# A decoder layer in float32: the bias of attention's output as one more product of TensorE

## The chip, the cores and the metric

The kernel runs on one core of a Trainium2 chip. Its time is the device time of one execution in microseconds. Before the change three runs took 5265.96, 5266.59 and 5273.14 us; the median, 5266.59, is what the changed kernel is compared with. The engines are named as in the profile: PE is TensorE (its weight loads are PEld), DVE is VectorE, ACT is ScalarE, POOL is GpSimd, SP is SyncE, whose queue issues most transfers.

## The reference, cut to what matters

```python
x = layernorm(x + mamba(x))                       # selective scan, 1024 channels, 16 states
x = layernorm(x + attention(x, ctx, mask))        # 16 heads of 32
x = layernorm(x + experts(x))                     # 32 routed experts and a shared MLP

# the end of attention, for each of 8 batches (512 rows of 512)
out = out.transpose(0, 2, 1, 3).reshape(B, L, D_MODEL)
return out @ Wo.T + bo
```

All is float32. x has 8 batches of 512 rows and 512 columns. In the mamba part, dt = softplus(dt @ dt_proj_w + dt_proj_b) with dt of rank 32, and dt_proj_w is 32 x 1024. The values' bias bv of attention adds a constant row to every row of the attention result, since the softmax weights of a row sum to one; so the kernel leaves bv out of the values and adds bv @ Wo.T to bo once.

## The kernel before, in words

The function `layers` computes the first two parts and the routing, `experts` the routed experts, `finish` the last layernorm. The change is all in `layers`.

The scan runs chunk by chunk: 16 chunks of 256 rows, two to a batch, 32 steps to a chunk. A step takes four channel groups of a state group: DVE multiplies (`steps_in`, L494, 128x1024), scans (`scan`, L501) and multiplies by C (`collect`, L510); ACT makes the decays ahead (`decays`, L480, four activations, a quartet, into one of two buffers `das`); PE folds the states (`products`, L521) into `py`, begun by a product with the identity (L519), and DVE gates the result (`gated`, L535). Six `h` buffers go round: a new step's L494 needs the fold products of the sixth step before it. Beside these steps other work is placed: the projections of the next chunk (`project`, L343), its convolution (L363 and L369 on ACT, L377 on DVE), the dt product (`prepare`, L437, with `w_dt`), x_proj (L400), and attention, routing and shared MLP of the batch before (`units`).

`units(b)` lists the parts of attention for batch b with weights, and the step loop takes them from the list in proportion, so that the attention of batch b lies beside the scan of batch b+1. A part is a product on PE and a rest that follows on another engine when the next part has been issued. The framework's scheduler then fixes the order of the instructions on each engine when the program is built; each engine works its own list in order. The last batch's attention stands alone behind the scan.

The part that the change touches is `output(lt)`, four for each batch. `dense` makes a 128x512 product of four 128x128 pieces of `attT` and `Wo` (L756) in one of two PSUM buffers. Then DVE adds the residual (L919, into `xr`) and the bias, which has been broadcast to all 128 partitions (L920, into `x2t`). After the fourth, layernorm 3 follows: statistics on DVE (L62, L63, L65), a logarithm and an exponential on ACT (L69, L70), a Newton step on DVE (L74 to L79), and the normalization on ACT (L81). PE transposes the result (`flip2`, L932), ACT copies it (L933), and the products of the shared MLP (L756, from `x2T`) and of the router (L588) follow. The residual rows are fetched two tiles ahead of use into two buffers `xr`.

Once, near the start (step 2 of the first chunk), `biases` makes bv @ Wo.T: L1051 repeats bv, L1052 multiplies, and L1055 adds the product to `bo`, which L278 has loaded with a broadcast to 128 partitions. SP's queue at that time issues, in this order: the spill of B and C (`scr`, L408), the clearing of the experts' buffer `xbuf` (L258, 1.36 MB each, one of many), the broadcasts of B and C (`bc`, L418), the repeats of dt and of dt times x (`rep`, L428).

Of the kernel before, what the change touches and what calls it, by code (L numbers as in the profile page):

```python
# [8 lines left out]
F32 = mybir.dt.float32  # L9
# [3 lines left out]
ALU = mybir.AluOpType  # L13
# [4 lines left out]
P = 128  # L18
B, S, D = 8, 512, 512
DC = D // P  # L20
# [3 lines left out]
DI = 1024  # L24
# [65 lines left out]
def layers(ctx, tc, a, x1d, filld, based, xbuf, arm):  # L90
# [42 lines left out]
    def const(name, shape, src):  # L133
        t = cp.tile(shape, F32, name=f"l_{name}")
        nc.sync.dma_start(t, src)
        return t
# [40 lines left out]
    cw = const("cw", [P, CC, 4], rows(a["conv_w"]))  # L177
    cb = const("cb", [P, CC], a["conv_b"])
    w_x = const("w_x", [P, CC, RANK + 2 * NST], rows(a["x_proj_w"]))
    w_dt = const("w_dt", [RANK, DI], a["dt_proj_w"])  # L180
    b_dt = const("b_dt", [P, CC], a["dt_proj_b"])
    dpar = const("dpar", [P, CC], a["D_param"])
    rs = const("rs", [P, 1], a["res_scale"].partition_broadcast(P))
    bq = cp.tile([P, DC], F32, name="l_bq")
    bk = cp.tile([P, DC], F32, name="l_bk")
    bv = cp.tile([P, DC], F32, name="l_bv")
    bo = cp.tile([P, D], F32, name="l_bo")
    wg = cp.tile([P, DC, E], F32, name="l_wg")

    aneg = cp.tile([P, CC, NQ, NG], F32, name="l_aneg")  # L190
# [72 lines left out]
    def later_constants():  # L263

        nc.sync.dma_start(
            aneg.rearrange("p c j g -> p (c j) g"),
            a["A_log"].rearrange("(b c) (s g) -> (c s) b g", c=QP, s=NQ),
        )
        for i in range(NPB):
            for r0 in (HD + 1, 2 * HD + HD + 1):  # L270
                nc.sync.dma_start(
                    kas[i][r0 : r0 + 1, :].rearrange("p (c t) -> p c t", c=DC),
                    ones[0:1, :].unsqueeze(1).to_broadcast([1, DC, P]),
                )
        nc.sync.dma_start(bq, a["bq"])
        nc.sync.dma_start(bk, a["bk"])
        nc.sync.dma_start(bv, a["bv"].rearrange("(c p) -> p c", p=P))
        nc.sync.dma_start(bo, a["bo"].partition_broadcast(P))  # L278
        nc.sync.dma_start(wg, rows(a["wg"]))


# [150 lines left out]
    def prepare(q, f):  # L432

        ps = psm.tile([P, 2, T], F32, tag="mm", name="ps_dt")
        for i in range(2):
            c = 2 * q + i
            nc.tensor.matmul(  # L437
                ps[:, i, :], w_dt[:, c * P : (c + 1) * P], f["xd"][0:RANK, :], start=True, stop=True
            )

        def exponentials():
            u = mp.tile([P, 2, T], F32, tag="u", name="u")
            dt = mp.tile([P, 2, T], F32, tag="dt", name="dt")

            for i in range(2):
                c = 2 * q + i
                nc.scalar.activation(u[:, i, :], ps[:, i, :], AF.Abs, bias=b_dt[:, c : c + 1])
                nc.scalar.activation(dt[:, i, :], ps[:, i, :], AF.Relu, bias=b_dt[:, c : c + 1])
            nc.scalar.activation(u, u, AF.Exp, scale=-1.0)
            l = mp.tile([P, 2, T + 3], F32, tag="xp", name="l")[:, :, 0:T]  # L450
            nc.scalar.activation(l, u, AF.Ln, bias=1.0)
            w = dtx = mp.tile([P, 2, T], F32, tag="dtx", name="dtx")
            nc.scalar.activation(w, u, AF.Identity, bias=1.0)

            def both():

                nc.vector.scalar_tensor_tensor(w, w, -1.0, u, ALU.add, ALU.subtract)
                nc.vector.tensor_tensor(l, l, w, ALU.subtract)
                nc.vector.tensor_tensor(dt, dt, l, ALU.add)
                nc.vector.tensor_tensor(dtx, dt, f["xs"][q], ALU.mult)  # L460
                f["ready", q] = dt, dtx
                return wait(timesD)

            def timesD():
                for i in range(2):
                    c = 2 * q + i
                    nc.scalar.activation(
                        f["xs"][q][:, i, :], f["xs"][q][:, i, :], AF.Identity, scale=dpar[:, c : c + 1]
                    )

            return wait(both)

        return exponentials
# [276 lines left out]
            todo.append((3.4, lambda j=j: keys(j), False))  # L750
        return todo

    def dense(lhs, rhs):
        ps = psm.tile([P, S], F32, tag="mm", name="ps_p")
        for dc in range(DC):
            nc.tensor.matmul(ps, lhs(dc), rhs(dc), start=(dc == 0), stop=(dc == DC - 1))  # L756
        return ps

    def units(b):
# [148 lines left out]
        def output(lt):  # L908
            if lt == 0:
                st["x2t"] = big("s1", "x2t").rearrange("p (j r) -> p j r", j=SC)  # L910
                st["x2"] = [st["x2t"][:, j, 0:D] for j in range(SC)]
            xr = st.pop(("xr", lt))
            if lt + 1 < SC:
                fetch(lt + 1)
            w, attT = loaded["Wo"], st["attT"]
            pp = dense(lambda dc: attT[:, dc, lt * P : (lt + 1) * P], lambda dc: w[:, dc, :])

            def add_up():
                nc.vector.tensor_tensor(xr, pp, xr, ALU.add)  # L919
                nc.vector.tensor_tensor(st["x2"][lt], xr, bo, ALU.add)  # L920
                if lt == SC - 1:
                    return layernorm(nc, sm, st["x2"], st["x2"], "ln3")

            return add_up
# [112 lines left out]
    def biases():  # L1037
# [12 lines left out]
        for dc in range(DC):  # L1050
# [1 line left out]
            nc.tensor.matmul(  # L1052
                psb, rep[:, dc * P : (dc + 1) * P], loaded["Wo"][:, dc, :], start=(dc == 0), stop=(dc == DC - 1)
            )
        nc.vector.tensor_tensor(bo, bo, psb, ALU.add)  # L1055

    chunks = [(b, t) for b in range(B) for t in range(S // T)]
    steps = [(q, g, jj) for q in range(CC // 2) for g in range(NG) for jj in range(2)]
# [584 lines left out]
```

## Time and profile before

| what | us |
|---|---|
| median of three runs | 5266.59 |
| the profiled execution | 5280.81 |
| its span | 5279.1 |
| scan phase, first step to the last scan | 58 to 3521 |
| attention, routing and shared MLP of the last batch, alone | to about 3800 |
| experts | about 3800 to 5240 |
| PE busy over the span | 4501.0 (85%) |
| DVE busy | 4173.3 (79%) |
| ACT busy | 2586.6 (49%) |
| L919, 32 adds | 21.8, 680 ns each |
| L920, 32 adds | 21.7, 678 ns each |

A row of the timeline gives the start, the time, the engine, the line, the operation, what it writes and reads, and how many instructions were merged; in square brackets stands the idle time of the engine before it and what ended it. PE records a float32 product twice: 128 products of `wa` and `attT` are 256 records. The answer by windows gives the busy time of each engine in a stretch and the share of full speed that PE's clock was granted.

### The profile page before, as it was taken

How to read it: one execution, taken by the hardware profiler on the slowest of the kernel's cores; microseconds unless marked ns; L12 is line 12 of the kernel's file. 1: busy time of each engine (PE TensorE's matmuls, PEld its weight loads, DVE VectorE, ACT ScalarE, POOL GpSimd, SP SyncE). 2: the span in 40 equal slices, each digit the busy share in tenths (PEclk: the TensorE clock that was granted, in tenths of full speed). 3: DMA queues.
4: the chain of work that ended last, by engine and by line, in shares of the span. 5: the costliest groups of instructions: out<-in, count | busy, mean ns of one | idle time of the engine just before them, and what ended most of it. 6: DMA issues, size and time to landing. Idle time of an engine off the chain costs nothing. (4 is left out here: it accounts for less than half of the span.)

```text
span 5279.1 us, 54371 instructions
## 1 busy us (share of the span) xinstructions
PE 4501.0 (85%) x17184; PEld 2464.4 (47%) x17184; DVE 4173.3 (79%) x5351; ACT 2586.6 (49%) x5771; POOL 588.5 (11%) x426
## 2 busy tenths in 40 slices
PE   6768889888888888888897888888899999999995
PEld 3324234333433433343342343332478888877774
DVE  7999898989989898998999899874355666656555
ACT  5565565665656556565655556533122333323233
POOL 1000002002000200200020020010112121111111
PEclk8879899999999999999999999999899999999997
DMA  8885345435533634544463554432244444444444
GB/s 236 266 229 157 72 119 177 115 101 148 160 95 91 208 88 109 171 128 102 105 201 78 125 173 113 106 115 93 93 129 125 128 139 132 128 116 132 117 123 151
DMA packets 486438, 711.64 MB, mean 135 GB/s; under 512 B 121576, under 2 KB 205064, under 8 KB 483952
## 3 DMA queue, kind: packets, MB, share of 16 engines
q1 hardware_dynamic: 449984, 626.90, 41.0%
q0 software_dynamic: 33280, 67.81, 5.8%
q10 hardware_dynamic: 2736, 11.54, 0.5%
q8 instruction: 221, 3.62, 0.3%
q14 instruction: 217, 1.78, 0.1%
HBM read 391.24 MB, written 164.79 MB: 105 GB/s over the span
## 5 line engine op out<-in xcount | busy, mean ns | idle before, releaser
L480 ACT ACTIVATE l_da<-rep,l_aneg 128x256 f32<-128x256 f32 x2048 | 893.5, 499 | 950.0 <-DVE h L501 885.6
L501 DVE TENSOR_TENSOR_SCAN h<-l_da,h 128x1028 f32<-128x1028 f32 x512 | 1163.3, 2285 | 21.6 <-ACT l_da L480 19.1
L494 DVE TENSOR_TENSOR h<-rep,bc 128x1024 f32<-128x1024 f32 x512 | 612.3, 1212 | 109.1 <-PE py L521 91.2
L510 DVE TENSOR_TENSOR h<-h,bc 128x1024 f32<-128x1024 f32 x512 | 616.8, 1211 | 2.1
L521 PE MATMUL py<-h,l_fold 128*32 128x512 f32 x2048 | 371.9, 649 | 108.1 <-DVE h L510 89.7
L819 PE MATMUL ps_s<-l_ka,l_qa 64*128 64x512 f32 x1024 | 331.8, 719 | 134.5 <-DVE mx L821 134.2
L1334 PE MATMUL ps_h<-xT,w 128*128 128x224 f32 (+3 forms) x1536 | 380.0, 397 | 38.4 <-issue 31.4
L1427 POOL DMA_INDIRECT based<-y,xe x160 | 272.5, 1703 | 1168.5 <-ACT y L1406 439.1
L821 DVE TENSOR_REDUCE mx<-ps_s 128x2 f32<-128x1024 f32 x256 | 309.8, 1214 | 67.8 <-PE ps_s L819 67.4
L861 PE MATMUL po<-eT,l_va 128*64 128x512 f32 x1024 | 302.5, 672 | 49.0 <-ACT eT L849 44.2
L1334 PEld LDWEIGHTS ps_h<-xT,w 128*128 128x128 f32 x1536 | 295.4, 193 | 103.8 <-issue 46.7
L845 PE MATMUL ps_t<-l_qa,l_ka 64*128 64x512 f32 x1024 | 305.5, 668 | 23.5 <-ACT eT L849 23.2
L849 ACT ACTIVATE eT<-ps_t 128x1024 f32<-128x1024 f32 x256 | 258.7, 1014 | 127.9 <-PE ps_t L845 127.8
L694 POOL DMA_INDIRECT xbuf<-x2t,dest x128 | 217.1, 1696 | 864.6 <-DVE dest L679 763.9
L343 PE MATMUL ps_z<-xnT,wm 128*128 128x256 f32 x1024 | 237.9, 389 | 28.4 <-DVE o L561 24.2
L756 PE MATMUL ps_p<-x2T,wa 128*128 128x512 f32 x512 | 241.9, 627 | 21.8 <-ACT hT L950 15.5
L552 PE MATMUL po<-wm,zs 128*128 128x512 f32 x512 | 248.5, 640 | 13.1 <-DVE z L963 11.8
L1334 PE MATMUL ps_h<-t,s 128*128 128x224 f32 (+3 forms) x1024 | 248.1, 393 | 5.8 <-DVE hT L1355 5.8
L1355 DVE TENSOR_TENSOR hT<-ps_h,p 128x224 f32<-128x224 f32 (+3 forms) x128 | 55.2, 432 | 248.9 <-PE ps_h L1334 248.8
L343 PE MATMUL ps_x<-xnT,wm 128*128 128x256 f32 x1024 | 245.7, 392 | 5.0 <-ACT xnT L332 3.2
L343 PEld LDWEIGHTS ps_z<-xnT,wm 128*128 128x128 f32 x1024 | 195.2, 193 | 90.2 <-DVE o L561 37.4
L343 PEld LDWEIGHTS ps_x<-xnT,wm 128*128 128x128 f32 x1024 | 195.8, 195 | 80.2 <-issue 43.7
(239 smaller groups left out, 6989.4 us busy)
## 6 DMA issues: line engine op xcount, KB each, us to landing
w<-in_w SPq DMA_DIRECT2D x93, 1024.0 KB
wm<-in_in_proj_w SPq DMA_DIRECT2D x128, 512.0 KB
rep<-dt SPq DMA_DIRECT2D x256, 256.0 KB
rep<-dtx SPq DMA_DIRECT2D x256, 256.0 KB
xbuf<-zero SPq DMA_DIRECT2D x32, 1362.5 KB
xe<-xbuf SPq DMA_DIRECT2D x32, 1362.5 KB
wm<-in_out_proj_w SPq DMA_DIRECT2D x64, 512.0 KB
wa<-in_sw SPq DMA_DIRECT2D x24, 1024.0 KB
```

Source lines behind the costliest of these rows:

```text
L343: nc.tensor.matmul(ps[:, i, :], w[:, dc, i * P : (i + 1) * P], f["xnT"][:, dc, :], start=(dc == 0), stop=(dc == DC - 1),)
L480: nc.scalar.activation(da[:, n, 1:], dt[:, j, i, :], AF.Exp, scale=aneg[:, 2 * q + i, 2 * jj + j, g : g + 1])
L494: nc.vector.tensor_tensor(h[:, :, 1:], dtx.rearrange("p j i t -> p (j i) t"), f["bc", g][0], ALU.mult)
L501: nc.vector.tensor_tensor_scan(flat, da.rearrange("p n t -> p (n t)"), flat, 0.0, ALU.mult, ALU.add)
L510: nc.vector.tensor_tensor(h[:, :, 0:T], h[:, :, 1:], f["bc", g][1], ALU.mult)
L521: nc.tensor.matmul(f["py"][j * QP : (j + 1) * QP, :, :], fold, hs[j // 2][:, 2 * (j % 2) : 2 * (j % 2) + 2, 0:T], start=False, stop=g == N ...
L819: nc.tensor.matmul(ps[:, j, :], qa[r, lt * P : (lt + 1) * P], ka[r, :], start=True, stop=True)
L821: return lambda: nc.vector.tensor_reduce(mx[:, lt, :].unsqueeze(2), ps, AX.X, ALU.max) and None
L845: nc.tensor.matmul(ps[:, j, :], ka[r, kc * P : (kc + 1) * P], qa[r, :], start=True, stop=True)
L861: nc.tensor.matmul(po[j * 2 * HD : (j + 1) * 2 * HD, :], va[:, kc, i, j * HD : (j + 2) * HD], eT[:, j, :], start=(kc == 0), stop=(kc == SC ...
L1334: nc.tensor.matmul(ps, w[:, n, r * P : (r + 1) * P], x[:, n, 0:cols], start=not more and n == 0, stop=n == 1, skip_group_check=more,)
L1427: put = nc.gpsimd.indirect_dma_start(out=based, out_offset=bass.IndirectOffsetOnAxis(ap=xe.bitcast(I32)[:, j, D + E :], axis=0), in_=ys[j] ...
```

## The change

The bias is no longer kept on 128 partitions. `w_dt`, the tile of dt's weights, grows from 32 to 64 partitions: the upper 32 hold dt's weights as before, the first of the lower 32 holds the bias of attention's output in 512 of its columns, and the other 31 are zero. In `dense`, a fifth product is added for the output: 32 rows of ones as the stationary operand and the 32 rows of bias and zeros as the moving one, accumulated into the same PSUM buffer. The add of the bias on DVE goes, and the residual add writes `x2t` directly. In `biases` the sum of bo and bv @ Wo.T is made on one partition of a buffer, and a transfer brings it to its row of `w_dt`, since DVE's lanes don't change partitions.

```diff
-    w_dt = const("w_dt", [RANK, DI], a["dt_proj_w"])
+    w_dt = cp.tile([2 * RANK, DI], F32, name="l_w_dt")
+    nc.sync.dma_start(w_dt[0:RANK, :], a["dt_proj_w"])
+    bo = w_dt[RANK : 2 * RANK, 0:D]
+    nc.gpsimd.memset(bo, 0.0)
...
-    bo = cp.tile([P, D], F32, name="l_bo")
...
-        nc.sync.dma_start(bo, a["bo"].partition_broadcast(P))
...
-                ps[:, i, :], w_dt[:, c * P : (c + 1) * P], f["xd"][0:RANK, :], start=True, stop=True
+                ps[:, i, :], w_dt[0:RANK, c * P : (c + 1) * P], f["xd"][0:RANK, :], start=True, stop=True
...
-    def dense(lhs, rhs):
+    def dense(lhs, rhs, row=None):
         ps = psm.tile([P, S], F32, tag="mm", name="ps_p")
         for dc in range(DC):
-            nc.tensor.matmul(ps, lhs(dc), rhs(dc), start=(dc == 0), stop=(dc == DC - 1))
+            nc.tensor.matmul(ps, lhs(dc), rhs(dc), start=(dc == 0), stop=(dc == DC - 1 and row is None))
+        if row is not None:
+            nc.tensor.matmul(ps, ones[RANK : 2 * RANK, :], row, start=False, stop=True)
         return ps
...
-            pp = dense(lambda dc: attT[:, dc, lt * P : (lt + 1) * P], lambda dc: w[:, dc, :])
+            pp = dense(lambda dc: attT[:, dc, lt * P : (lt + 1) * P], lambda dc: w[:, dc, :], bo)
 
             def add_up():
-                nc.vector.tensor_tensor(xr, pp, xr, ALU.add)
-                nc.vector.tensor_tensor(st["x2"][lt], xr, bo, ALU.add)
+                nc.vector.tensor_tensor(st["x2"][lt], pp, xr, ALU.add)
...
-        nc.vector.tensor_tensor(bo, bo, psb, ALU.add)
+        row = p3.tile([P, D], F32, tag="row", name="bo")[0:1, :]
+        nc.sync.dma_start(row, a["bo"].unsqueeze(0))
+        nc.vector.tensor_tensor(row, row, psb[0:1, :], ALU.add)
+        nc.sync.dma_start(bo[0:1, :], row)
```

## The prediction

> **What bounds the kernel now.** I read the chain of waits first; it only follows the last experts' transfers and the closing layernorm, after 5187 us, which the change doesn't touch. So I went on to the busy time by stages.
>
> ```profile
> core 0: us, PE busy (x) PEld busy (x) DVE busy (x) ACT busy (x) POOL busy (x), PEclk, DMA share, GB/s
> 58.00:460.00 402.00, 285.08 (x840) 121.90 (x840) 399.68 (x366) 240.87 (x591) 21.48 (x12) 0.79 0.79 231
> ...
> 1665.00:2118.00 453.00, 381.81 (x1381) 165.59 (x1381) 411.32 (x453) 266.92 (x595) 41.31 (x29) 0.94 0.47 129
> ...
> 3467.00:3700.00 233.00, 202.77 (x702) 74.97 (x700) 121.14 (x172) 76.93 (x119) 16.28 (x19) 0.92 0.32 105
> ```
>
> DVE bounds the scan phase: 91% busy in a full batch period (411.3 of 453 us) and 99% in the first, which has no attention output yet. After 3520 PE bounds. The output product of attention (lines 913 to 921) runs eight times: at 761, 1212, 1665, 2118, 2570 and 3023 us inside full periods, at 3467 near the end of the scan, at 3712 alone. Next, one of the six in the timeline, and the PE lines that give prices:
>
> ```profile
> 1666.31 0.68 DVE L920 TENSOR_TENSOR x2t<-xr,l_bo 128x512 f32<-128x512 f32 x1
> 1666.77 7.13 PE L756 MATMUL ps_p<-wa,attT 128*128 128x512 f32 x16
> 1666.91 0.68 DVE L919 TENSOR_TENSOR xr<-ps_p,xr 128x512 f32<-128x512 f32 x1
> ...
> 1671.33 0.69 DVE L919 TENSOR_TENSOR xr<-ps_p,xr 128x512 f32<-128x512 f32 x1 [0.74 <-DMA xr<-x1d]
> ...
> 1673.74 3.62 PE L343 MATMUL ps_x<-xnT,wm 128*128 128x256 f32 x16
> ...
> 1677.29 1.06 PE L521 MATMUL py<-h,l_fold 128*32 128x512 f32 x6
> ...
> 1683.49 0.16 DVE L74 TENSOR_TENSOR m<-v,r 128x4 f32<-128x4 f32 x1 [1.45 <-ACT r L70]
> ...
> 1687.36 2.93 ACT L81 ACTIVATE x2t<-x2t,less,r 128x512 f32<-128x512 f32 x4 [1.71 <-DVE less L79]
> 1688.22 1.97 PE L932 MATMUL ps_tr<-l_ident,x2t 128*128 128x128 f32 x8 [8.03 <-ACT x2t L81]
> ...
> 1695.66 3.60 PE L756 MATMUL ps_p<-x2T,wa 128*128 128x512 f32 x8
> 1699.10 3.65 PE L588 MATMUL ps_l<-l_wg,x2T 128*128 128x32 f32 x32
> ```
>
> See that PE stands idle for 8.03 us until layernorm 3 has normalized x2t; DVE, working through adds, statistics and scan steps in between, is what is late. And the eighth output, with nothing beside it:
>
> ```profile
> 3710.29 10.55 PE L756 MATMUL ps_p<-wa,attT 128*128 128x512 f32 x20 [3.73 <-DVE attT L900]
> ...
> 3717.44 0.69 DVE L919 TENSOR_TENSOR xr<-ps_p,xr 128x512 f32<-128x512 f32 x1 [1.11 <-PE ps_p L756]
> ...
> 3720.88 0.69 DVE L919 TENSOR_TENSOR xr<-ps_p,xr 128x512 f32<-128x512 f32 x1 [1.07 <-PE ps_p L756]
> 3721.60 0.69 DVE L920 TENSOR_TENSOR x2t<-xr,l_bo 128x512 f32<-128x512 f32 x1
> ```
>
> Here DVE waits for each product: PE is on the path.
>
> **Removed: 32 adds on DVE.** L920 starts at 1666.31 and the next instruction at 1666.91, so one takes 0.60 us of a full DVE queue (0.68 overlaps the next), four 2.4 us per output. xr is free one instruction earlier, so its next load (the 0.74 us wait) should no longer be waited for.
>
> **Added: 32 products on PE.** Each float32 product shows as two records (256 records for the 128 products of wa and attT). Eight such records take 1699.10 - 1695.66 = 3.44, so 0.43 each, and a product of 128x512 is 0.86; depth does not help (the 32-row products of L437 show 374 ns at 128x256, as L343's do). A change of array shape costs extra: 16 half-width records before L521 take 1677.29 - 1673.74 = 3.55 against 16 x 0.215 = 3.44, so 0.11. Into the 32-row shape and out: 0.86 + 0.22 = 1.08 us, 4.3 per output. Bounds: 0.86 with no price for the shape; above, L437's weight loads were preceded 52 times by an idle of 33.5 us in all that nothing ended ("issue" in the answer for that line), 0.64 each, so 0.86 + 1.28 = 2.14. I take 1.08, since L521 is the nearest row: a change of shape right behind 128x128 work.
>
> Against this change speaks the Trainium skill, TensorEngine Tiling (Array Packing), Key Properties: switching the tiling mode drains TensorE. The row agrees that switching isn't free, at 0.11. With the 166 ns constant of a warm matmul (TensorE: Matmul & The Clock Gate, Single matmul latency and the lines after) as the drain, an estimate is 1.19 per product, 4.8 per output instead of 4.3; the sum would move by 0.5 in the last output alone.
>
> **A full period, stepped through.** The order on each engine is fixed when the program is built; I use the changed program's order with the durations of this trace (1024-wide multiply 1.11, scan 2.2, convolution tap 0.40, statistics 0.60).
> PE: output 0 is whole at 1664.7, now with its bias at 1665.8; output 1 at 1667.9, output 2 at 1672.4, output 3 at 1676.9 (1673.7 before: four fold products, 1.0, move behind them). The 16 ps_x records end at 1680.4, then eleven fold products wait for nothing, to about 1684.
> DVE from 1665.3, in its new order: multiply (1666.4), add 0, tap, statistics, add 1 (1668.7, having waited 0.1 for PE), multiply, statistics, scan (1672.7), multiply, add 2 (1674.5), multiply, statistics, scan (1678.4), add 3 (1679.1), multiply, statistics, variance (1681.0; before 1681.2).
> ACT now has both quartets of decays ahead of the logarithm: second scan over at 1678.4, quartet 1.7, two table loads of 1.28 and two 0.2 activations: 1683.1, where it was 1683.5. DVE puts two multiplies into the Newton step and the taps behind it, so the shift `less` is out at 1686.2 instead of 1687.3: x2t starts 1.1 us earlier, and DVE has done 3 multiplies (3.3) more and 5 taps (2.0) less, so stands 1.1 + 1.3 = 2.4 us ahead. The gate of L535 comes at 1691.0 instead of 1694.0; PE's L519 waits for it, then the last transposes and their copy, so the shared MLP's first product starts at about 1693.4 instead of 1695.66: 2.2 ahead.
> I take 2.3 per period, six periods: -13.8. The lower bound is 1.1 (only x2t's lead survives), the upper 2.3 + 0.8 (see the transposes below).
> The 4.3 us on PE cost nothing here, because the 8.03 us wait hides them: PE is done at 1684, x2t comes at 1686.2. If that cover is used up, see rival 1.
>
> The wait also slows what follows it: eight L932 records take 1.97 us after the 8.03 us wait, and 1.14 at 3495.41, after 0.23. Whether the shorter wait cures that, no row shows: 0 to 0.8 per period, not in my sum. The skill's TensorE: Matmul & The Clock Gate, Part 1, has PE's clock halved after an idle window of about 3.4 us; with the 2 us left, that rule would add the whole 0.8 six times, a sum of -16.0 instead of -11.2.
>
> **The seventh output** (3467): DVE is ahead by the same 2.4, but the first add now waits about 1 us for the bias, and the order mixes in more scan steps; the gate logic ends earlier, x2t later. I take -1.5, from +2 (PE's lateness counts) to -4 (the scan's lead counts).
>
> **The eighth** (3712): four products of 1.08 go on the path, one add of 0.72 (3721.60 - 3720.88) off it, the other three adds lie in DVE's waits: +3.6; by the bounds +2.7 to +7.8.
>
> **The beginning.** The broadcast load of bo (256 KB) goes; a memset of 32x512 on POOL (0.55 by the neighbours of L241) comes, hidden, since POOL has nothing urgent until 16.7 us. Three steps are new on SP and DVE: the row's load stands behind the scr spill, needs filld's landing (issued at 33.99) and delays the xbuf clear and eight bc loads by one issue, 0.4; they themselves wait until 43.40 for scr. DVE's L1055 now waits for the row, and behind it is queued the product dtx whose transfers DVE idles for (10.41 us until 58.5). scr, issued at 39.55, let its readers go at 43.40; the row right behind it should land by 44, before L1055 is reached at about 46.7. The write-back to w_dt is issued behind all rep loads of that step, 0.5 on SP ahead of weight loads, and is read 700 us later. Without cover: the row's landing would go on the path, 1 to 3 us. The built order also differs in the first period, where DVE has only 2.3 us of slack in 402. I take +0.5 for all, -1 to +5.
>
> **Sum:** -13.8 - 1.5 + 3.6 + 0.5 = -11.2 us. The profiled execution took 5280.8, 14.2 above the median of 5266.6; taken off the median: **5255.4**.
>
> **Rivals.**
> 1. Slower: the bias product lands on the path in every period. Place: the last add, which DVE reaches at 1678.5. It decides from the price where output 3 is ready no earlier: 1673.7 - 1.0 + 4p = 1678.5, p = 1.45 us. For it: L437's 0.64 us gaps; PE is 84% busy, its slack in the new order is 2 us. Against: 0.11 at L521. At p = 2.14 output 3 comes 2.8 us late, the fold products as well, so h buffers are freed late: +0.5 net per period (2.8 - 2.3), +7.8 at the eighth, about +3 at the seventh: 3 + 3 + 7.8 + 0.5 = +14, 5281.
> 2. No gain that lasts: DVE's 9% idle time takes the place of the adds; the 2.4 us lead is lost at the next wait for PE's fold products (L494, 14.6 us in six waits in the list of waits of one period), because PE got 4.3 us more. For it: both engines are over 80% busy. Against: x2t and the MLP start earlier too. Time: 0 per period, +2.6 rest: 5269.
> 3. More than forecast: the transposes run in 1.14, so 3.1 per period, and -4 at the seventh: -18.6 - 4 + 3.6 + 0.5 = -18.5, 5248. For it: the shorter wait; against: PE's slack is used up by the bias.
> 4. The order of the first period costs DVE 5 us more, the rest as forecast: 5260.
>
> **How the numbers follow.** Forecast 0.48 (own range 5249 to 5261), rival 1 0.16, rival 2 0.15, rival 3 0.10, rival 4 0.11. No change is within 0.2%, 10.5 us, about what a measurement of this kernel can tell: 5256.1 to 5277.1. The forecast lies 0.7 us inside "faster"; I count two thirds of it there, since the transposes' gain is left out of it: 0.31, with rival 3 and a fifth of rival 4 0.43. Slower takes most of rival 1 (0.13) and a tail of rival 2 (0.03): 0.16. Same is the rest, 0.41. The range, 5246 to 5274, leaves out rival 1 and little else.
>
> **What would show it.** Right: 32 fewer DVE instructions in the scan phase, DVE busy 2.7 lower per period, output to output 450.5 instead of 453, PE's wait for x2t down from 8.03 to 2 or 3 us, two records of 32-row shape behind each output, and the eighth output's x2t 3.6 later after the first product. Wrong: the bias records with idle above 0.3 us before their weights; PE waits in DVE's list at L919; DVE idle in the first period above 2.3 us.

## The result, and the profile after

The changed kernel takes 5292.3 us in the median of five runs (5267.6 to 5299.6), where the kernel before took 5266.6 (5266.0 to 5276.5). The ratio is 1.0032, with a 95% interval of 1.0019 to 1.0045: slower by 10 to 24 us, 17 in the middle. The forecast was 5255.4, with a range up to 5274. Of the rivals, 1 (the products on the path in every period, 5281) came nearest in the number, though not at the place that it names, as the adds show below; 2 (no gain that lasts) gave 5269. The five runs lie 32 us apart, the fastest at a mean granted clock of 0.933 and the others at 0.927 to 0.930; both profiled executions had 0.928, so the mean clock doesn't make the difference between these two.

The span of the profiled execution went from 5279.1 to 5294.8, by 15.7. By the starts of DVE's first adds of each output, it comes about so:

| stretch | forecast | measured |
|---|---|---|
| start to the first output's first add | +0.5 | 760.9 to 765.8: +4.9 |
| five periods, to the sixth output | -11.5 | 3022.7 to 3030.0: +2.4 |
| the sixth period, to the seventh output | -2.3 | 3467.1 to 3480.3: +5.9 |
| seventh output, to the eighth | -1.5 | 3711.9 to 3728.5: +3.4 |
| eighth output, to the experts' first activation | +3.6 | +5.1 |
| experts and closing layernorm | 0 | -6.0 |

An output's first add stands behind its first bias product. For the eighth that matters: PE starts again behind its wait for `attT` 14.9 us later than before (3710.29 to 3725.14, in the rows below and in the prediction), the first add 16.6 later. Counted from PE's start, the stretch of the seventh lost 1.6 us and the eighth 6.9.

The last row's code is the same in both kernels, and it moved between -22 and +3 us in the profiles below. So single profiles are used here to find places, and the sizes are taken from the timed comparisons.

The busy time by stages after:

```profile
58.00:460.00 402.00, 277.41 (x842) 118.69 (x841) 396.84 (x363) 238.15 (x588) 18.35 (x12) 0.79 0.80 231
...
1665.00:2118.00 453.00, 392.75 (x1382) 166.68 (x1384) 408.55 (x449) 266.40 (x592) 40.17 (x29) 0.92 0.47 128
...
3467.00:3700.00 233.00, 206.71 (x681) 76.14 (x679) 125.59 (x175) 74.27 (x126) 16.23 (x19) 0.90 0.35 109
```

DVE has 2.8 us less to do in the full period (411.32 before), as forecast, but the period isn't shorter: it lasts 452.8 us in the mean of five, 452.4 before. In the first stretch DVE idles 5.2 us of 402, where it idled 2.3. One output region of after, the fourth, from the timelines of DVE, PE and ACT:

```profile
2125.42 0.69 DVE L922 TENSOR_TENSOR x2t<-ps_p,xr 128x512 f32<-128x512 f32 x1
...
2137.56 0.66 DVE L922 TENSOR_TENSOR x2t<-ps_p,xr 128x512 f32<-128x512 f32 x1
...
2142.38 0.16 DVE L74 TENSOR_TENSOR m<-v,r 128x4 f32<-128x4 f32 x1 [2.00 <-ACT r L70]
```

```profile
2127.05 3.70 PE L757 MATMUL ps_p<-wa,attT 128*128 128x512 f32 x8
2130.68 1.12 PE L759 MATMUL ps_p<-l_w_dt,l_ones 32*128 32x512 f32 x2
2131.73 3.70 PE L757 MATMUL ps_p<-wa,attT 128*128 128x512 f32 x8
2135.36 1.12 PE L759 MATMUL ps_p<-l_w_dt,l_ones 32*128 32x512 f32 x2
2136.42 3.72 PE L344 MATMUL ps_x<-xnT,wm 128*128 128x256 f32 x16
2140.07 2.77 PE L522 MATMUL py<-h,l_fold 128*32 128x512 f32 x22
2146.56 1.97 PE L934 MATMUL ps_tr<-l_ident,x2t 128*128 128x128 f32 x8 [3.72 <-ACT x2t L81]
...
2155.19 4.00 PE L757 MATMUL ps_p<-x2T,wa 128*128 128x512 f32 x8
```

```profile
2142.14 0.20 ACT L70 ACTIVATE r<-r 128x4 f32<-128x4 f32 x1
2142.25 0.57 ACT L364 COPY xp<-ps_x 128x512 f32<-128x512 f32 x1
```

Up to the transposes the forecast holds. In five of the six outputs inside full periods the four adds waited 0.06 us in all for PE; in the third, which met a halved clock, 2.2. ACT takes ps_x 2.1 us after they end (2136.42 + 3.72 = 2140.14, taken at 2142.25), since the new order puts the convolution behind the logarithm. PE's wait for x2t is down from 8.03 to 3.72 us. The transposes start 21.1 us after the first add, where they started 23.2 after it (2118.2 to 2141.4) before: a lead of 2.0. By the forecast's own figures it is 2.2, since its first add comes at 1666.4 instead of 1665.3 and x2t 1.1 earlier. The transposes themselves take 1.97 us behind the wait of 3.72 as they did behind 8.03, so the gain of rival 3 didn't come. The price of a product is read from two outputs in a row: 2131.73 - 2127.05 = 4.68 us for four products and the bias. Before, eight products without bias took 1673.74 - 1666.77 = 6.97, so 3.49 for four: 1.19 us for the bias.

Then the lead goes. The shared MLP's first product stands 29.8 us behind the first add (2125.42 to 2155.19), before 30.3 (1665.32 to 1695.66), by the forecast's figures 27.0 (1666.4 to 1693.4): of 3.3 us 0.6 came here, and 1.0 in the mean of the six periods. PE's clock stayed halved for longer there, as the column before the last two shows, after and before:

```profile
2151.00:2156.00 5.00, 5.00 (x11) 1.58 (x10) 5.00 (x5) 3.52 (x6) 0.00 (x0) 0.52 0.00 0
```

```profile
1692.00:1697.00 5.00, 4.11 (x16) 2.65 (x15) 5.00 (x6) 4.28 (x10) 0.00 (x0) 0.85 0.00 0
```

The list of DVE's waits over three periods (second to fifth output), before and after:

```profile
DVE h L494 <- PE py L521: 39.1, 17, 6.8
DVE m L74 <- ACT r L70: 15.4, 12, 2.9
```

```profile
DVE h L495 <- PE py L522: 44.2, 20, 5.5
DVE m L74 <- ACT r L70: 20.1, 12, 4.8
```

These two waits (us in all, times, longest) grew by 9.8 us, and the adds that went are worth 3 x 2.4 = 7.2. So far this is rival 2. Whether the products cause it, as rival 2 has it, only runs could tell.

The eighth output after, from PE's timeline, and the clock beside it (the column before the last two is the granted clock):

```profile
3725.14 1.31 PE L757 MATMUL ps_p<-wa,attT 128*128 128x512 f32 x2 [3.72 <-DVE attT L903]
3726.38 2.07 PE L759 MATMUL ps_p<-l_w_dt,l_ones 32*128 32x512 f32 x2
3728.38 2.08 PE L757 MATMUL ps_p<-wa,attT 128*128 128x512 f32 x2
3730.38 2.07 PE L759 MATMUL ps_p<-l_w_dt,l_ones 32*128 32x512 f32 x2
...
3742.57 1.12 PE L759 MATMUL ps_p<-l_w_dt,l_ones 32*128 32x512 f32 x2
```

```profile
3729.00:3734.00 5.00, 5.00 (x6) 1.34 (x5) 2.49 (x6) 0.00 (x0) 0.00 (x0) 0.50 0.21 52
...
3739.00:3744.00 5.00, 4.69 (x11) 1.67 (x10) 1.84 (x4) 0.00 (x0) 0.00 (x0) 1.00 0.05 9
```

After PE's wait of 3.72 us the clock is halved for some 10 us, and two of the four products fall into it: 2.07 us instead of 1.12. Before, behind a wait of 3.73 us at the same place, it was halved too, but for some 3.4 us:

```profile
3711.00:3716.00 5.00, 5.00 (x10) 1.93 (x9) 3.97 (x7) 0.00 (x0) 0.00 (x0) 0.68 0.18 52
```

### The profile page after: what moved, and what is told of

It is laid out like the page before. It is cut to its first block, busy times and chain, and to the rows that moved or that the text cites. A ratio compares the mean times of both kernels' runs of the same rounds, so it can differ in the third digit from the quotient of the medians.

```text
span 5294.8 us, 54485 instructions
## 1 busy us (share of the span) xinstructions
PE 4555.4 (86%) x17248; PEld 2472.4 (47%) x17248; DVE 4158.6 (79%) x5319; ACT 2591.0 (49%) x5771; POOL 588.2 (11%) x427
## 5 line engine op out<-in xcount | busy, mean ns | idle before, releaser
L502 DVE TENSOR_TENSOR_SCAN h<-l_da,h 128x1028 f32<-128x1028 f32 x512 | 1166.3, 2291 | 21.5 <-ACT l_da L481 18.6
L864 PE MATMUL po<-eT,l_va 128*64 128x512 f32 x1024 | 299.8, 666 | 48.8 <-ACT eT L852 44.2
```

The lines of the kernel that those rows point to most:

```text
L502: nc.vector.tensor_tensor_scan(flat, da.rearrange("p n t -> p (n t)"), flat, 0.0, ALU.mult, ALU.add)
L864: nc.tensor.matmul(po[j * 2 * HD : (j + 1) * 2 * HD, :], va[:, kc, i, j * HD : (j + 2) * HD], eT[:, j, :], start=(kc == 0), stop=(kc == SC ...
```

## The experiments

All sizes below are ratios to the kernel before on the same chip, with 95% intervals; 0.1% is 5.3 us. Line numbers differ from kernel to kernel.

### Parts of the change, each ordered anew

```diff
 # without the product: the changed kernel, and
-            pp = dense(lambda dc: attT[:, dc, lt * P : (lt + 1) * P], lambda dc: w[:, dc, :], bo)
+            pp = dense(lambda dc: attT[:, dc, lt * P : (lt + 1) * P], lambda dc: w[:, dc, :])
 # zero product: the kernel before, and
+            nc.tensor.matmul(ps, ones[RANK : 2 * RANK, :], zrow, start=False, stop=True)
 # row early: the changed kernel, with the row's load moved up
+        nc.sync.dma_start(bo_in, a["bo"].unsqueeze(0))     # in later_constants
 # POOL: the kernel before, and
             nc.sync.dma_start(xr, x1d[b * S + j * P : b * S + (j + 1) * P, :])
+                nc.gpsimd.tensor_tensor(xr, xr, bo, ALU.add)
```

> The changed kernel without the 32 bias products: the beginning as changed (4.8 us late at 285 us in the trace of after), the adds gone from DVE, the bias left out of the sum. Theory A (the products take back on PE what DVE gained): the removal alone is worth the 2.3 us a period that were forecast, so 5266.6 + 4.8 - 13.8 - 1.5 - 0.7 = 5255, 37 below after. Theory B (fewer adds on DVE are worth nothing in the full periods, because DVE waits longer for PE and ACT later on): 5266.6 + 4.8 - 0.7 = 5271, within 3 of the beginning's loss; outputs a period apart by 452 to 453 us as before.

Measured: 1.0027 (1.0014 to 1.0041), 14 us slower. Both theories fall: the kernel without the products is no faster than before.

> The kernel before with one more product for each output, of 32 rows of zeros, and both adds kept on DVE: PE's part alone, the beginning as before. Theory A: four products of 1.1 us a period cost about 2.8 in each of six periods (0.5 measured against -2.3 forecast), 3 at the seventh output and 4.4 to 7 at the eighth: 5266.6 + 17 + 3 + 6 = 5292. Theory B: PE's products lie in its 8 us wait for x2t and cost only at the last two outputs: 5266.6 + 3 + 6 = 5276.

Measured: 1.0091 (1.0076 to 1.0105), 48 us slower: more than either theory.

> The changed kernel with the row of bo loaded where the broadcast load stood before, so that DVE's add in biases does not wait for its landing. Theory A (the 4.8 us that after is late by 285 us begin with this wait, and stay to the end): dtx no more than 1 us late at 47 us, outputs 2 to 5 us earlier than in after, 5288 to 5290. Theory B (the late start comes from the order of the first chunk, or is absorbed later): 5291 to 5293, the first output still 4 to 5 us later than before.

Measured: 1.0027 (1.0013 to 1.0041). The first dtx is 2.8 us late (3.6 in after), and at 394 us the scan is 4.9 late, as in after (4.8). The row's wait isn't what costs the beginning.

> The kernel before with the bias added to the residual rows on POOL behind their load, so that DVE has one add an output and PE no product; the beginning as before. Theory A: DVE's part alone is worth 2.3 us a period: 5266.6 - 13.8 - 1.5 - 0.7 = 5251. Theory B: worth nothing in the periods: 5266. Slower, above 5272, if POOL's add (not in any trace so far) makes the residual rows later than the product, or holds up DVE.

Measured: 1.0057 (1.0043 to 1.0072), 30 us slower. POOL's add takes 1.27 us, and DVE waited 14.6 us in all for residual rows that POOL had not finished.

None of the four answers, because each has another order: the framework's scheduler makes the order when the program is built, and any change of the work makes a new one, up to 140 us behind the edit. One thing was common to them and to after. Taken from the period's first scan step and over four periods, DVE's scan steps at 138 us behind the output stood 4 to 6 us later than in the kernel before, whatever had been added or removed. Part of that is no loss, since the new orders start ahead: counted from the scan step 32 us before the output to 130 us behind it, in the mean of six periods, after loses 1.2 us, the four between 0.9 and 4.3.

### The order held

So the order of the kernel before was recorded for each engine, and given to the variants as dependencies that bind only the issue. All instructions but those of the edit stand exactly as before:

```diff
+def hold(tc, new):
+    ...
+            for i in [*ahead[seq[k].name], seq[k], *behind.get(seq[k].name, [])]:
+                if last is not None:
+                    tc.add_manual_dep(i, last.name, NoSync, reason="recorded order")
+                last = i
```

> The kernel before with the second add left out (so the bias is left out of the sum), and every engine's instructions held in the order of the kernel before. In the first experiments each kernel was ordered anew by the framework's scheduler, and lost 3 to 6 us a period between 66 and 140 us behind the output, whatever it had added or taken away. Theory C (that loss is the new order's, not the work's): with the order held, less work can't cost: 2 to 15 us below before, by my forecast for DVE's part 13.8 + 1.5 + 0.7 = 16 at most. Theory D (fewer adds make DVE run into PE's fold products and ACT's layernorm earlier, in any order): 5 to 10 us above before, as without the product in the first experiments.

> The change itself (bias product on PE, one add on DVE) with everything else in the order of the kernel before, each product right behind its four, and the beginning as before (bo still broadcast, its first row copied to the tile of dt's weights). Theory C: my forecast without the beginning's 0.5, 11.7 below before, or, if the lead is lost at the next wait, 3 above (the eighth output alone). Theory D: as the changed kernel without its 4.8 us at the start, 12 above before.

> PE's part alone in the order of before: both adds kept, one more product of zeros for each output. Theory C: the eighth output pays 4.4, the seventh up to 3, the six in the periods 0 to 0.5 each since PE waits 8 us for x2t: 4 to 10 above before. Theory D: 48 above, as the same work had in its own order.

> The work of before in the order of after: no product, two adds for each output (the second with a tile of zeros; the bias is left out), all else in the order that the changed kernel has, its beginning too. Theory C: the order's loss alone, 4.8 at the start and 2 to 3 a period: 5 to 25 above before. Theory D: before plus the 4.8 of the start at most.

Measured, with what the changed kernel has in its own order:

| work | order of before | order of after |
|---|---|---|
| two adds, no product | 1 | 1.0057 (1.0044 to 1.0070), +30 us |
| one add, no product | 0.9983 (0.9974 to 0.9992), -9 us | not run |
| two adds, product | 1.0077 (1.0064 to 1.0090), +41 us | not run |
| one add and product: the change | 1.0071 (1.0058 to 1.0084), +37 us | 1.0032 (1.0019 to 1.0045), +17 us |

Theory C holds for the add: DVE's part gains 9 us once the order is held, and the new order costs by itself, a little more than the 25 that it allowed. It falls for the products: held, they cost all that they take, 32 x 1.19 = 38 us against 41 measured. Theory D came near there (48), but not for the change as a whole (12, measured 37). The new order costs 30 with the old work, and it is the better one for the new work (17 instead of 37). So two things can cost here, a new order and, in the order of before, a product that isn't hidden; the first four runs mix them.

Where the products cost is seen in what the add of the held change waited for (the answer for its line), beside the run without products and the kernel before:

```profile
its engine sat idle before it (us, times) until:
  PE ps_p L846: 55.3, 32
```

```profile
its engine sat idle before it (us, times) until:
  DMA xr<-x1d: 13.2, 7
  PE ps_p L841: 8.3, 5
```

```profile
  PE ps_p L756: 6.2, 4
  DMA xr<-x1d: 5.6, 6
```

With the products every one of the 32 adds waits for PE. And the wait goes on from there. ACT's timeline in the kernel before, then ACT, PE and DVE in the run with products of zeros:

```profile
1677.67 0.57 ACT L363 COPY xp<-ps_x 128x512 f32<-128x512 f32 x1
1678.57 1.09 ACT L369 ACTIVATE xs<-xp,l_cb,l_cw 128x256 f32<-128x256 f32 x2
...
1680.44 1.28 ACT L69 ACT_TABLE_LOAD   x1
```

```profile
1686.79 0.59 ACT L451 COPY xp<-ps_x 128x512 f32<-128x512 f32 x1 [1.97 <-PE ps_x L431]
...
1687.88 1.09 ACT L457 ACTIVATE xs<-xp,l_cb,l_cw 128x256 f32<-128x256 f32 x2
...
1689.07 1.28 ACT L69 ACT_TABLE_LOAD   x1
```

```profile
1696.86 1.97 PE L1022 MATMUL ps_tr<-l_ident,x2t 128*128 128x128 f32 x8 [8.35 <-ACT x2t L81]
```

```profile
1678.38 0.69 DVE L1009 TENSOR_TENSOR xr<-ps_p,xr 128x512 f32<-128x512 f32 x1 [1.99 <-PE ps_p L846]
```

In before, PE's ps_x, which follow the fourth output, end at 1677.36 (1673.74 + 3.62), and ACT, done with its decays, takes them at 1677.67. That margin is 0.3 us here, and 0.3 to 0.8 in the six full periods. The convolution stands in ACT's queue ahead of the logarithm of layernorm 3, so x2t follows ps_x as it follows the adds. With the products ACT waits 1.97 us for ps_x, in each of the six. PE still waits its 8 us for x2t: 8.35. The wait that was taken for cover is the length of a chain that begins with PE's own last product; make the block longer, and the wait moves along with it.

### The same products behind the block

> The kernel before in its own order with both adds, and the same four products of zeros for each batch, but put into the wait itself: behind the last fold product and right ahead of the transposes that wait for x2t, into a PSUM buffer that nobody reads. Theory E (x2t waits for a chain that begins at PE's own block of outputs and ps_x; PE time costs inside that block and is free behind it): 0 to 4 above before. Theory F (PE is short of time as a whole, 36 us more of it cost 36 wherever they stand): 30 to 40 above before, as the same products inside the block, which cost 37.

```diff
+                spare = pss.tile([P, 2, S], F32, tag="sc", name="ps_spare")[:, 0, :]
+                for n in range(4):
+                    nc.tensor.matmul(spare, ones[RANK : 2 * RANK, :], row_bo, start=(n == 0), stop=(n == 3))
             ps = psm.tile([P, DC, P], F32, tag="mm", name="ps_tr")
```

Measured: 1.0016 (1.0007 to 1.0025), 8 us, where the same products inside the block cost 41. Theory F falls: PE as a whole isn't short of time. E is right in kind; it gave 0 to 4, and where the rest comes from stays open. PE's timeline shows the products in the wait:

```profile
1674.22 3.69 PE L435 MATMUL ps_x<-xnT,wm 128*128 128x256 f32 x16
...
1682.25 3.70 PE L1024 MATMUL ps_spare<-l_w_dt,l_ones 32*128 32x512 f32 x8
1690.36 1.97 PE L1028 MATMUL ps_tr<-l_ident,x2t 128*128 128x128 f32 x8 [4.41 <-ACT x2t L81]
```

### A shorter product, and the wait for the residual rows

The bias is cut into three rows of bfloat16 (its upper part, the upper part of the rest, and what is left), which one product with ones adds up:

```diff
+        nc.gpsimd.tensor_copy(thirds_h[0:1, :], left_f)
+        nc.gpsimd.tensor_tensor(left_f, left_f, thirds_h[0:1, :], ALU.subtract)
+        nc.gpsimd.tensor_copy(more_h, left_f)
+        nc.sync.dma_start(thirds_h[1:2, :], more_h)
+        nc.gpsimd.tensor_tensor(left_f, left_f, more_h, ALU.subtract)
+        ...
+            nc.tensor.matmul(ps, ones_h, row, start=False, stop=True)      # row: the three rows, bfloat16
```

> The change in the order of before, with the bias cut into three rows of bfloat16 that add up to it exactly, so that each product is one bfloat16 instead of a float32 product of two records. By the rows so far, half a record pair or less: 0.2 to 0.5 us instead of 1.12. Theory E with a cost in proportion to the price: the float32 products cost 48 against the run without them, so 9 to 21, less the 10 that the adds are worth: from 1 below to 11 above before. If only what goes beyond a margin costs (0.3 us between ps_x's end and its copy on ACT in before): down to 10 below before.

Measured: 0.9988 (0.9979 to 0.9997), 6 us faster than before: between the two theories, nearer to the one with the margin. In its timeline two outputs in a row are 3.94 us apart, so the product costs 3.94 - 3.49 = 0.45:

```profile
2115.87 3.70 PE L853 MATMUL ps_p<-wa,attT 128*128 128x512 f32 x8
2119.50 0.38 PE L855 MATMUL ps_p<-l_w_dt 32*128 32x512 bf16 x1
2119.81 3.70 PE L853 MATMUL ps_p<-wa,attT 128*128 128x512 f32 x8
```

Against the run without any product, 32 x 0.45 = 14 us of product cost 3 (0.9983 to 0.9988, and the intervals overlap), where 32 x 1.19 = 38 us cost 46 (0.9983 to 1.0071). The trace doesn't show a margin that the short products fit into: ACT waited 0.5 to 1.7 us for ps_x in each of the six full periods, and 15 of the 32 adds waited for PE. The start of the experts on ACT, in the run without products (span 5267.1) and with the short ones (5261.5), shows more:

```profile
3797.51 0.43 ACT L1433 COPY p<-ps_h 128x320 f32<-128x320 f32 x1 [46.94 <-PE ps_h L1419]
```

```profile
3809.01 0.43 ACT L1456 COPY p<-ps_h 128x320 f32<-128x320 f32 x1 [45.93 <-DVE s L1394]
```

Up to here the short products cost 11.5 us in the profiles, near the 14 that they take, and the long ones 43. Behind it the run with the short ones takes 17 us less (1452.5 instead of 1469.6, 1474.5 in before), in code that is the same in all. That is so in all four profiles with bfloat16 rows, 16 to 22 us below before in the experts and the closing layernorm; the other fifteen lie between 11 below and 3 above. Why the experts run shorter with these rows stays open, and with it whether the 6 us are worth anything in the layers: the profiles speak for the theory with a cost in proportion to the price.

> The same three bfloat16 rows, ordered by the framework's scheduler. Theory C (each new order costs by itself, 27 in the order of after with the old work): 5 to 30 above before, whatever the products cost. If a new order is fitted to its work and costs nothing: as the held run with bfloat16, within 5.

Measured: 1.0015 (1.0006 to 1.0024), 8 us slower than before and 14 slower than the same work held. Theory C, at the lower end.

> The run without the second add in the order of before, with a third buffer for the residual rows (the bias's tile is left out to make room, and the bias with it). There DVE came 0.6 us earlier and waited 2.04 us for the third residual row where before had waited 0.74. If that wait swallowed the rest of DVE's gain: 6 times up to 1.4 more, 14 to 18 below before. If another wait stands behind it (ps_x, the decays or the scan): 10 below, as with two buffers.

```diff
-            st["xr", j] = xr = p2.tile([P, D], F32, tag="xr", name="xr")
+            st["xr", j] = xr = p2.tile([P, D], F32, tag="xr", name="xr", bufs=3)
```

Measured: 0.9987 (0.9978 to 0.9996), the same as with two buffers. The reason isn't the one in the second theory: the wait itself stayed (13.9 us in seven waits, 13.2 with two buffers), so it isn't the buffer that the load waits for. SP's timeline points at its own queue: at the third output it issues the loads of the residual rows at 1665.63, right behind two repeats of dt that occupy it from 1663.75 (1667.02 behind 1664.87 in before), and this order was held. A run with these loads moved up wasn't made.

### Which stretch of the new order

> The changed kernel as it is, with one part of its order put back: in each of the six full periods everything from 25 us behind the output's first add on (router, shared MLP, back projection) stands in the order of before; the outputs themselves, the start and the end stay in the new order. In after the transposes of x2t stand 2.0 us ahead, as forecast, and the lead is lost between 66 and 140 us, in the waits for PE's fold products. Theory G (the new order of that stretch loses the lead): 2 us a period kept instead of 0.5 lost, so 10 to 17 below after, level with before to 7 above. Theory H (the products on PE use the lead up wherever the rest stands): as after, 17 above before.

> The changed kernel with only the part from 95 us on (back projection, layernorm 2) of each full period in the order of before. Theory G, if the waits for the fold products behind the back projection are the loss: 6 to 15 below after. If the loss was made earlier, in the MLP between 25 and 95 us: as after, 17 above before.

> As the run with the order put back from 25 us on, with the first chunk in the order of before as well. By the traces the new order of the first chunk costs 2.5 of the 4.8 us at 394 us, the row's wait the rest: 2 to 4 below that run, so 3 below to 5 above before by theory G; 13 above by theory H.

> The three rows of bfloat16 in that mixed order (start and everything from 25 us on as before, the outputs in the new order). By theory G the six periods keep 2 to 3 us each, and the last two outputs lose 2 instead of 10 together: 8 to 18 below before, and below the 6 that the bfloat16 rows gained in the order of before. By theory H, or if the new order of the outputs only fits the long products: 0 to 6 below before.

How the orders were joined, in outline (the kernels hold only the joined lists):

```diff
+    for sa, sb in stretches(after[e], before[e]):      # in which the two orders differ
+        if start[e][sa] - output >= T:                 # T: 25 us, or 95
+            after[e][sa:sb] = before[e][sa:sb]
```

From 95 us on, the two orders differ only on DVE and ACT; PE's list is the same there.

Measured: 1.0088 (1.0075 to 1.0101), 1.0080 (1.0067 to 1.0093), 1.0095 (1.0082 to 1.0108), and 1.0025 (1.0012 to 1.0038) with bfloat16. The first three are slower than after, and the last is slower than the same work held, so theory G falls in this form, and H with it. Two things were seen in the traces. Cut at 25 us, the run loses 3 to 4 us between the transposes and the router in each period, since the new order of the outputs and the old order behind them don't meet. And in the last two periods of all four, ACT's instructions beside the outputs had slipped into the order of before as well. PE and ACT there, in the run with the back projection restored:

```profile
2597.87 1.97 PE L1025 MATMUL ps_tr<-l_ident,x2t 128*128 128x128 f32 x8 [13.09 <-ACT x2t L81]
```

```profile
2583.09 0.29 ACT L580 COPY h<-l_state 128x4 f32<-128x4 f32 x2 [13.99 <-PE py L613]
```

ACT stood 14 us for a fold product that the new order of PE puts behind all outputs, and PE's wait for x2t became 13.09 instead of 3.72. That slip shows how much an order of one engine is worth without the other's. It also means that these four runs don't settle what they were made for. The next one is the second of them without the slip:

> The run with the back projection's order put back, mended: there, in the last two of the six periods, ACT's instructions beside the outputs had slipped into the order of before too (convolution ahead of the logarithm), and x2t came 6 us later in each of them. Here only the part from 95 us on is in the order of before, in all six periods. In the undisturbed three periods of that run's trace the 2.5 us that after loses between 110 and 156 us are kept. Theory I (they stay to the next output): six times 2.5 below after, 2 above before. Theory J (they are lost again before the next output, as another wait stands behind): that run's 39 less two times 6 and no more, 15 to 27 above before, no better than after.

Measured: 1.0029 (1.0018 to 1.0040), the same as after. Theory J: between 110 and 156 us nothing is lost any more, and the next output is no earlier. Where the order of after loses its 30 us stays open; putting back this one stretch doesn't recover them.

> The same order with the three rows of bfloat16 in place of the float32 product, and the first chunk in the order of before. Theory I: 10 to 20 below before, better than the 6 that these rows gain in the order of before. Theory J: between 0 and 15 above before, as the new orders with these rows had so far (8 and 13).

Measured: 0.9968 (0.9956 to 0.9981), 5258.9 us in the median against 5271.5 of before in the same runs: 17 us faster than before, and 34 faster than the changed kernel by its own ratio. Theory I gave 10 to 20, but not by its reason, since the float32 run beside it gained nothing. What differs between the two is the product, the first chunk's order, and that of SP and POOL, which is that of before. It is the fastest version that keeps the bias. By its profile most of the gain lies where the code is the same, as with the other bfloat16 rows: the experts start 4 us earlier than in before and take 16 less. So these 17 us are measured, but that they come from the order or from the product isn't shown.

## Why the prediction was wrong, step by step

**The period, -13.8: the step that failed.** It is "I take 2.3 per period, six periods". A lead, found by stepping through 30 us of the new order, was taken as a lead at the next output. Measured, five periods took 2.4 us more than before, where 11.5 less was forecast. The lead at the transposes came (2.0 of 2.2 by the forecast's figures), at the MLP's first product 1.0 of 3.3 was left. The new order differs from the old for 110 us more, and that part was not stepped through. What the forecast left out is the price of the order itself: the old work in the new order lost 30 us.

Rival 2 named a place, the waits for fold products. In the three periods of the lists above the old work in the new order waited 38.6 us for them and 19.4 for r, before 39.1 and 15.4, after 44.2 and 20.1: so the longer wait for r goes with the order, the longer one for fold products with the new work. Rival 2's reason, that PE got 4.3 us more, isn't confirmed by that: the run without products ended no better in its own order, and it waited 46.7 us for fold products. In the new order, going from the old work to the new is worth 30 - 17 = 13 us, near the forecast of 11.2. That is no confirmation: the forecast's terms miss one by one, and both sizes are uncertain by 7 us.

"The 4.3 us on PE cost nothing here, because the 8.03 us wait hides them" was said of the new order, and at the outputs of after it looks right: the adds waited 0.06 us, and PE was done with its fold products at 2142.84 and had 3.72 us left until x2t. Whether the products cost something later in that order isn't known, since the new order without them was run only with two adds. Its reason fails, though. In the order of before, where the wait of 8.03 us was read, the products inside the block cost 41 us, and in the wait 8. The wait was read from the idle time ahead of PE's next instruction. What had to be read was when the results of PE's block were needed: by the adds (32 of 32 waited) and by ACT's copy of ps_x (0.3 to 0.8 us of margin). The new order had moved that copy behind the logarithm; the forecast has the decays ahead of the logarithm, but doesn't name the copy.

**The residual row.** "xr is free one instruction earlier, so its next load should no longer be waited for": refuted. DVE came earlier, and the load did not: the waits for it grew from 5.6 us (six) in before to 13.2 (seven) in the held run without the add. That growth of 7.6 us is about what is missing: DVE's part is worth 9 us instead of the 16 in its expectation. No run took the wait away, so this is argued and not shown.

**The price, 1.08.** Mis-sized: 1.19 in a full period. Rival 1's point of decision, 1.45, was not reached, and in after the last add of a period waited for PE in none of the six, as that rival has it below 1.45. That its 5281 came near is luck. In the order of before, for which it wasn't worked out, the products did land on the path in every period. The estimate from the Trainium skill (TensorEngine Tiling (Array Packing), Key Properties: a switch of the tiling mode drains TensorE), 1.19 with the constant of a warm matmul, agrees with what was measured; whether the 0.32 us beyond the 0.87 of a 128x512 product are a drain, no run shows. The idle time that I had named as a sign, above 0.3 us ahead of the weights, came (27.3 us in 32), but beside PE's work, so it is no sign of the price.

**The beginning, +0.5.** Mis-sized: 4.9. Rival 4 (DVE loses 5 us to the first period's order) is right in place and near in size. In single profiles the scan at 394 us was 4.8 late in after and 4.9 with the early row, but 2.2 with the first chunk in the order of before and the start else as changed; runs that keep the broadcast of bo lie between 0.1 and 2.9 there.

**The seventh output, -1.5, and the eighth, +3.6.** Measured +3.4 and +5.1 between first adds, and 1.6 and 6.9 from PE's start at the eighth. So counted, both lie inside their bounds (-4 to +2, 2.7 to 7.8), and neither value held. At the eighth four products of 1.19 less one add of 0.72 make 4.0. PE's block took 18.6 us (3725.14 to 3743.69) instead of 10.55, which is 3.2 more than the products' 4.8: the clock stayed halved for some 10 us, where before it did for 3.4. The Trainium skill has the halving (TensorE: Matmul & The Clock Gate, Part 1: the clock is halved after an idle window of some 3.4 us). The trace agrees here, 0.50 behind a wait of 3.72 us, though not everywhere, as the last section says. The forecast weighed it for the transposes only, where with 3.72 us left instead of 2 they stayed at 1.97. Before had the same halving behind the same wait, so the rule by itself adds nothing at the eighth; that the half speed lasted three times as long has no explanation here. Nor has the +5.9 of the sixth period.

**What was right.** 32 fewer instructions and 2.8 us less on DVE in a period; PE's wait for x2t down to 3.72 (2 or 3 forecast); the sign of DVE's part; the last output slower.

## What to carry to other kernels

An engine's idle time covers added work only if the work stands behind whatever that wait is waiting for: follow the chain that ends the wait back, and if it begins with the same engine's last results, the cover is the margin of those results at their readers, here 0.3 to 0.8 us and not 8. Where a scheduler makes the order, an edit is two changes: measure it once with the old order held, before anything is said of the work. A term added on TensorE in float32 to a long float32 product can go in as a few bfloat16 rows that add up to it: here at 0.45 us a product instead of 1.19. What that was worth depended on the order, 6 and 17 us faster than before in two, 8 and 13 slower in two, and part of it came in a stage with the same code; so look where a gain lies before you call it the edit's.

## What the runs showed of the hardware that was not expected

- A product of 32 rows in bfloat16 behind float32 products costs 0.45 us, in float32 1.19, though both are 512 columns wide.
- The clock's half speed doesn't need a long wait of PE. In after it came behind a wait of 3.72 us in the eighth output, and also in the third (0.50 from 1672 to 1677 us) behind one of 1.22, and not in the fourth (1.00 from 2121 to 2141) behind one of 0.58. It lasted some 10 us in the eighth output, although PE was busy all of 3729 to 3739.
- The experts' stage, with the same code in every kernel, took 16 to 22 us less than before in the four profiles with bfloat16 rows in the layers, and from 11 less to 3 more in the fifteen others.
- POOL's add of 128x512 took 1.27 us, and DVE's adds in that run kept their 0.69.
